# Gathers of a chunk set three tiles apart, and the slots of an element worked out three half products sooner, in a routed feed-forward kernel

## The chip, the cores and the metric

The kernel runs on one core of a Trainium2 chip. The metric is device time in microseconds (us) of one execution. The engines are PE (TensorE: products and transposes; PEld is its weight load), DVE (VectorE), ACT (ScalarE), POOL (GpSimd, which issues the gathers and scatters) and SP (SyncE, which issues most other transfers). A letter q behind an engine's name means its queue of issued transfers. Transfers of all queues are carried out by 16 DMA engines.

## The reference

For 16 elements (b) of 512 tokens by 512 numbers, a conditioned layer with a GELU is followed by a routed feed-forward layer. Each token goes to the 4 of 16 experts (blocks of 128 hidden units) with the largest router values; their results are added to the token and to a bias.

```python
def _L0_cond_ref(x, u, v, b, W, fc_bias):
    z1 = jnp.einsum('bfi,bir->bfr', x, v[:, 0]) / inch
    z = jnp.einsum('bfr,bor->bfo', z1, u[:, 0]) / r
    y = jnp.einsum('bfi,oi->bfo', x, W) + fc_bias + z + b
    return jax.nn.gelu(y, approximate=False)
...
prob = jax.nn.softmax(xf @ w_router + b_router, axis=-1)
_, idx = jax.lax.top_k(prob, TOP_K)
mask = (idx[:, :, None] == jnp.arange(N_BLOCKS)[None, None, :]).any(axis=1)
...
h = jax.nn.relu(jnp.einsum('nd,ebd->neb', xf, w1b) + b1b[None])
y = jnp.einsum('neb,ebd,ne->nd', h, w2b, mask)
y = y + b2[None, :]
...
x = x + _L0_ffn_ref(_L0_cond_ref(...), ...)
```

All of it is in float32.

## The kernel before

**What is stored where.** Every expert has a list of rows in `g_d` (device memory). A token's activated row, 512 numbers, is written into the lists of its four experts at positions called slots; results come back to the same slots of `y_d`. A slot is known once the router's choice is ranked among all earlier tokens.

**First stage (lines 758 to 773).** `window(b)` (L578) runs once for each of the 16 elements. It consists of eight half products, `cond_half(b, h)` (L255): two of the four products that make one quarter of the conditioned layer for element b; after each odd one ACT applies the GELU into `gT`. Between the halves stand other pieces of work, listed by half in `do[h]`:

- for element b+1: `weights` (L233, PE products `pw` and four DVE additions `we`), and four times `turn_x` (L245: four PE transposes into `ptx`, copied by DVE into `xT`);
- for element b+2: `spread_v`, `turn_v` and `turn_v_out` (PE transposes `pu`, copied by DVE and ACT), and the load of its x, which can start when the last `turn_x` of element b has read the buffer;
- for the element before, a = b-1: `logits_in` (L281, products `pa`, copied by ACT into `parts`), `logits` (L291, `pl`), `route_in` (L298: DVE, then the exponential on ACT), `route` (L307: some twenty small DVE operations from `sm`, L318, to `acc`, L350), `turn_g` for each of its four chunks of 128 tokens (L353: transposes `ptg`, copied into `gr` by DVE for odd chunks, by ACT for even ones), `rank` (L413: three small products `pp`, which need `acc`) and `place` (L427: DVE operations that end in `slot`, L441);
- in windows 5, 6, 7, 9 and 13 to 15 chores of DVE (`fill`, `count`, `take`, `table_ahead`, `table_part`), which count the lists' tiles and are put at halves 1, 3 and 6;
- two scatters `put` (L445) of a quarter of a chunk's rows each, which POOL issues. There are 16 for an element. In window b they belong to element b-2, and each waits for the half product before it.

Each engine works through its instructions in this order. `ptx`, `ptg` and half of `pw` share two PSUM buffers, so a transpose waits until the one two before has been copied. `gr` has two buffers for each chunk.

**Second stage (lines 782 to 798).** The lists are read as 271 full or partly full tiles of 128 rows. Step i fetches tile i+4 (L631, SP), turns tile i+1 (L649, copied by ACT into `gs`, L650), does the first product of tile i (L656, then ACT's `h`, L660) and the second of tile i-1 (L666, copied by ACT into `y`, L667, stored by SP, L668), and picks the weights of tile i+2 (L643, DVE). The first 22 tiles (`AHEAD`) are known to be full from the first elements alone, and can be read while later rows are still being put; tile 22 and all later ones wait for all puts, and for five scatters of zeros (`put_zero`, L499) that fill the ends of the lists. The puts that the first stage didn't do, and the zeros, are planned into the first steps (L751 to L755).

**The way back.** The tokens of an element come back in four chunks of 128, 64 chunks in all. `begun(b, c)` (L677) says after how many tiles a chunk's rows have all been worked out: with n = 4b+c+1, max(38, 4n+15). A chunk needs four gathers `get_y` (L690, POOL, 256 KB each, into two halves `yg`), a load of x (L682, issued by ACT, into one of 11 buffers), an addition of the bias (L707), two additions for each half (L710, L714), and a store (L717, SP). `plan(step, ...)` puts each behind a step, counted from `at`: the gathers at `at` to `at+3`, the load at `at-24`, the bias at `at+3`, the four additions at `at+4` to `at+7`, the store at `at+7`. POOL is not held to the steps: it issues a gather as soon as its turn has come, the stores of the chunk's tiles have landed and a `yg` buffer is free (there are six, so three chunks' worth). SP, ACT and DVE issue theirs in the place that the plan gives.

Of the kernel before, what the change touches and what calls it, by code (L numbers as in the profile page):

```python
# [19 lines left out]
TOP_K = 4  # L20
# [5 lines left out]
def adaln_ffn_kernel(  # L26
# [31 lines left out]
    B, S, D = x.shape  # L58
# [3 lines left out]
    NC = S // P  # L62
# [29 lines left out]
    def alone(ins):  # L92

        tc.declare_no_dep(ins.ins, group="put_g", reason="disjoint rows of the lists")
        tc.declare_no_dep(ins.ins, group="get_g", reason="the tiles that run ahead are full")
        tc.add_to_no_dep_group("put_g", ins.ins)
# [158 lines left out]
    def cond_half(b, h):  # L255

        o = h // 2
        if h % 2 == 0:
            pms[o] = ps_m.tile([P, S], F32, tag="m", name=f"pc_{b}_{o}")
        for k in range(h % 2 * ND // 2, (h % 2 + 1) * ND // 2):  # L260
            ins = nc.tensor.matmul(  # L261
                pms[o], lhsT=wes[b][:, k, o * P : (o + 1) * P], rhs=xTs[b, k], start=(k == 0), stop=(k == ND - 1)
            )
        if h % 2:
            gelu(b, o, pms[o])
        return ins
# [178 lines left out]
    def put(b, c, j, after):  # L445

        ins = nc.gpsimd.indirect_dma_start(  # L447
            out=g_d[:, :],
            out_offset=bass.IndirectOffsetOnAxis(ap=slot[:, b, c, j : j + 1], axis=0),
            in_=grs[b, c].bitcast(I32),  # L450
            in_offset=None,
        )
        tc.add_manual_dep(ins.ins, after.ins.name, SYNC, reason="spread over the products")
        alone(ins)
        if b < Q:
            early.append(ins.ins)
# [42 lines left out]
    def put_zero(i, after):  # L499
        ins = nc.gpsimd.indirect_dma_start(  # L500
            out=g_blocks if i else g_d[:, :],
            out_offset=bass.IndirectOffsetOnAxis(ap=zero_i[:, i : i + 1], axis=0),
            in_=(zero if i else zero[:, 0:D]).bitcast(I32),
            in_offset=None,
            bounds_check=NSLOT // ZB - 1 if i else NSLOT - 1,
            oob_is_err=False,
        )
        tc.add_manual_dep(ins.ins, after.ins.name, SYNC, reason="spread over the products")
        alone(ins)
# [65 lines left out]
    for k in range(known):  # L575
        chores.setdefault(B - 2 + k // 3, []).append(parts_of[k])

    def window(b):  # L578
        a = b - 1
        do = [[] for _ in range(2 * ND)]  # L580
        if b + 1 < B:
            do[0] += [(weights, b + 1)]
            do[2] += [(turn_x, b + 1, 0), (turn_x, b + 1, 1)]
            do[4] += [(turn_x, b + 1, 2), (turn_x, b + 1, 3)]
            if b > 0:
                do[1] += [(logits_in, a)]
                do[3] += [(logits, a), (route_in, a)]
                do[4] += [(route, a)]
                do[5] += [(turn_g, a, 0), (turn_g, a, 1)]
                do[6] += [(turn_g, a, 2), (turn_g, a, 3)]  # L590
                do[7] += [(rank, a), (place, a)]
            if b + 2 < B:
                do[2] += [(spread_v, b + 2)]
                do[5] += [(turn_v, b + 2), (turn_v_out, b + 2)]
        else:
            do[0] += [(logits_in, a)]
            do[1] += [(logits, a), (route_in, a)]
            do[2] += [(turn_g, a, 0), (turn_g, a, 1), (route, a)]
            do[3] += [(turn_g, a, 2), (turn_g, a, 3)]
            do[5] += [(rank, a), (place, a)]  # L600
        for h, what in zip((1, 3, 6), chores.get(b, ())):
            do[h] += [what]
        for h in range(2 * ND):
            ins = cond_half(b, h)
            for what, *args in do[h]:
                what(*args)
            if b > 1:
                for j in (0, 1):
                    put(b - 2, h // 2, h % 2 * 2 + j, ins)
            if later:  # L610
                what, *args = later.pop(0)
                what(*args)
# [4 lines left out]
    rows, gts, wcs, gss, hTs, mark, stores = {}, {}, {}, {}, {}, {}, []  # L617
# [59 lines left out]
    def begun(b, c):  # L677

        n = b * NC + c + 1
        return max(AHEAD + E, n * PB // NC + E - 1)  # L680
# [40 lines left out]
    GAP = 3  # L721
# [4 lines left out]
    def plan(step, *what):  # L726
        work.setdefault(step, []).append(what)

    for b in range(B):
        for c in range(NC):  # L730
            at = max(begun(b, c) + GAP, at + TOP_K if b + c else 0)
            k = b * NC + c
            soon = FREE - 2 * XA + 2 * k if k < XA else FREE + 4 + k - XA
            plan(soon if k < XA + XB else max(at - 24, soon), load_x, b, c)
            for j in range(TOP_K):
                plan(at + j, get_y, b, c, j)
            plan(at + LAND, sum_b, b, c)
            for h in range(2):
                plan(at + LAND + 1 + 2 * h, sum_y, b, c, h)
                plan(at + LAND + 2 + 2 * h, sum_x, b, c, h)  # L740
            plan(at + LAND + 4, store, b, c)


    z = B - 1
    for step, *what in (
        (-1, logits_in, z), (0, logits, z), (0, route_in, z), (1, turn_g, z, 0), (1, turn_g, z, 1), (1, route_a, z),
        (2, route_b, z), (2, turn_g, z, 2), (3, route_c, z), (3, turn_g, z, 3), (4, rank, z), (5, place, z),
        (6, count, B // Q - 1), (7, ends), *((8 + k, *w) for k, w in enumerate(parts_of[known:])), (8 + NTC, table, 1),
    ):
        plan(step, *what)  # L750
    for i in range(NC * TOP_K):  # L751
        for k, b in enumerate((z - 1, z)):
            plan(8 * k + i // 2, lambda b, c, j: put(b, c, j, mark[0]), b, i // TOP_K, i % TOP_K)
    for i in range(1 + NZ):
        plan(16 + i // 3, lambda i: put_zero(i, mark[0]), i)  # L755

    ENG = mybir.EngineType
    with tc.manual_schedule(engines={ENG.PE, ENG.DVE, ENG.Activation}):
# [10 lines left out]
        for b in range(B):  # L769
            if 2 <= b + 2 < B:  # L770
                load(b + 2)
            window(b)
# [76 lines left out]
```

## Time and profile before

| | |
|---|---|
| three timed runs | 1089.81, 1096.34, 1098.36 us |
| median | 1096.34 us |
| the profiled execution, its own time | 1086.83 us |
| its span, first to last instruction | 1085.1 us |
| mean granted TensorE clock | 0.967 |
| busy share of the span: PE, DVE, ACT, POOL | 89%, 60%, 48%, 51% |
| moved, mean | 342.43 MB, 316 GB/s |
| second products (tiles) | 271 |
| scatters and gathers of POOL | 256 and 256, and 5 of zeros |
| first tile transposed | at 387.21 us |
| last second product ends | at 1049.69 us |

The page's second part cuts the span into 40 slices of about 27 us; a digit is a busy share in tenths.

```profile
PE   5998988988999888789799999999999999999960
DMA  9966667566654469988799999999999999999996
GB/s 301 332 230 216 224 215 261 208 225 242 226 223 179 170 224 318 358 265 272 259 382 405 394 388 403 391 394 395 395 397 401 395 396 398 380 405 398 392 354 211
```

The first stage is slices 1 to 14. From slice 21 on the transfers run at about 395 GB/s, until the last two slices. The profiled execution is one of several and was faster than the three timed ones; sums from the profile are made against its own time.

### The profile page before, as it was taken

What the parts mean: (1) busy time and instruction counts of PE and PEld (TensorE: products, weight loads), DVE (VectorE), ACT (ScalarE), POOL (GpSimd) and SP (SyncE); (2) the same over time, 40 slices, a digit from 0 to 9 for tenths busy, and PEclk for the clock granted to TensorE, in tenths of its full rate; (3) what the DMA queues carried; (4) which work ended last, traced back from release to release, by engine and by line L of the source; (5) the groups of instructions that cost most, each with busy time, mean ns of one, the idle gap of its engine ahead of it and who ended that gap; (6) DMA issues with size and microseconds to landing.
All of it is one profiled execution on the core that took longest, in us unless ns stands there. A gap on an engine that the chain in (4) does not pass through costs nothing.

```text
span 1085.1 us, 19007 instructions
## 1 busy us (share of the span) xinstructions
PE 970.9 (89%) x5320; PEld 639.3 (59%) x5320; DVE 648.0 (60%) x1450; ACT 518.8 (48%) x1006; POOL 550.3 (51%) x538
## 2 busy tenths in 40 slices
PE   5998988988999888789799999999999999999960
PEld 3544444544444455567577677677767777777740
DVE  4365667566556767323366666566666666666675
ACT  2333332342333434456466666566656566666640
POOL 2046666666666667500454445455444454444555
PEclk9999999999999988989899999999999999999985
DMA  9966667566654469988799999999999999999996
GB/s 301 332 230 216 224 215 261 208 225 242 226 223 179 170 224 318 358 265 272 259 382 405 394 388 403 391 394 395 395 397 401 395 396 398 380 405 398 392 354 211
DMA packets 161480, 342.43 MB, mean 316 GB/s; under 512 B 28723, under 2 KB 36951, under 8 KB 159046
## 3 DMA queue, kind: packets, MB, share of 16 engines
q1 hardware_dynamic: 110928, 188.53, 48.1%
q0 software_dynamic: 41856, 136.96, 33.6%
q10 hardware_dynamic: 8592, 15.73, 4.1%
q8 instruction: 44, 0.72, 0.3%
q14 instruction: 60, 0.49, 0.1%
HBM read 179.91 MB, written 163.32 MB: 316 GB/s over the span
## 4 chain that ended last, share of the span: by engine, by line
PE 58%; DMA 19%; DVE 8%; issue 5%; ACT 3%; POOL 2%; SPq 2%; another core or an unknown queue 2%; ACTq 1%; DVEq 0%; POOLq 0%
PE pc L261 17%; DMA gt<-g_d 14%; PE ph L656 14%; PE py L666 13%; PE pts L649 6%; PE ptx L248 2%; PE ptg L357 2%; PE pw L241 2%; PE pa L285 1%; ACT gs L650 1%; PE pl L294 1%; DVE xT L250 1%; DMA yg<-y_d,slot 1%; POOL g_d L447 1%
## 5 line engine op out<-in xcount | busy, mean ns | idle before, releaser
L694 POOL DMA_INDIRECT yg<-y_d,slot x256 | 283.1, 1106 | 338.0 <-DVE xr L715 163.8
L643 DVE COPY wcur<-wall 128x1028 f32 x271 | 193.0, 713 | 271.1 <-PE py L666 164.0
L447 POOL DMA_INDIRECT g_d<-gr,slot x256 | 254.3, 993 | 185.2 <-issue 65.8
L656 PE MATMUL ph<-gs,wcur 128*128 128x128 f32 x2168 | 293.7, 279 | 17.7 <-ACT gs L650 9.8
L666 PE MATMUL py<-wcur,h 128*128 128x512 f32 x542 | 281.2, 601 | 5.5 <-ACT h L660 4.8
L656 PEld LDWEIGHTS ph<-gs,wcur 128*128 128x128 f32 x2168 | 266.8, 194 | 26.6 <-ACT gs L650 17.4
L261 PE MATMUL pc<-xT,we 128*128 128x512 f32 x512 | 246.3, 608 | 0.0
L649 PEld LDWEIGHTS pts<-ident,gt 128*128 128x128 f32 x1084 | 134.9, 143 | 165.2 <-issue 108.8
L667 ACT COPY y<-py 128x512 f32<-128x512 f32 x271 | 159.2, 587 | 94.0 <-PE py L666 69.5
L650 ACT COPY gs<-pts 128x512 f32<-128x512 f32 x271 | 160.0, 590 | 85.0 <-DMA gt<-g_d 39.6
L649 PE MATMUL pts<-ident,gt 128*128 128x128 f32 x1084 | 165.6, 276 | 16.4 <-DMA gt<-g_d 14.3
L660 ACT ACTIVATE h<-ph,wcur 128x128 f32<-128x128 f32 x271 | 100.0, 369 | 89.6 <-PE ph L656 43.0
L261 PEld LDWEIGHTS pc<-xT,we 128*128 128x128 f32 x512 | 88.4, 192 | 88.7 <-issue 88.7
L270 ACT ACTIVATE gT<-pc,biasT 128x512 f32<-128x512 f32 x64 | 44.0, 688 | 158.0 <-PE pc L261 101.8
L712 DVE TENSOR_TENSOR yg<-yg 128x512 f32<-128x512 f32 x128 | 87.3, 682 | 8.2 <-DMA yg<-y_d,slot 6.8
L666 PEld LDWEIGHTS py<-wcur,h 128*128 128x128 f32 x542 | 83.2, 194 | 6.8 <-ACT h L660 5.1
L250 DVE COPY xT<-ptx 128x512 f32<-128x512 f32 x64 | 42.0, 686 | 60.4 <-PE ptx L248 27.8
L715 DVE TENSOR_TENSOR xr<-xr,yg 128x512 f32<-128x512 f32 x112 | 76.6, 684 | 0.0
L357 PE MATMUL ptg<-ident,gT 128*128 128x128 f32 x256 | 37.8, 281 | 27.1 <-issue 9.8
L357 PEld LDWEIGHTS ptg<-ident,gT 128*128 128x128 f32 x256 | 30.0, 143 | 50.5 <-issue 24.9
L243 DVE TENSOR_TENSOR we<-pw,wc 128x512 f32<-128x512 f32 x64 | 40.1, 683 | 23.9 <-PE pw L241 16.2
L248 PEld LDWEIGHTS ptx<-ident,x 128*128 128x128 f32 x256 | 31.3, 146 | 18.3 <-issue 14.9
(159 smaller groups left out, 511.2 us busy)
## 6 DMA issues: line engine op xcount, KB each, us to landing
gt<-g_d SPq DMA_DIRECT2D x271, 256.0 KB
y_d<-y SPq DMA_DIRECT2D x271, 256.0 KB
x<-in_x_dram SPq DMA_DIRECT2D x16, 1024.0 KB
xr<-in_x_dram ACTq DMA_DIRECT2D x56, 256.0 KB
out_dram<-xr SPq DMA_DIRECT2D x56, 256.0 KB
wall<-in_w1T_dram SPq DMA_DIRECT2D x16, 256.0 KB
wall<-in_w2T_dram SPq DMA_DIRECT2D x16, 256.0 KB
g_d<-gr,slot POOLq DMA_INDIRECT x256
```

The costliest lines, as they stand in the source:

```text
L261: ins = nc.tensor.matmul(pms[o], lhsT=wes[b][:, k, o * P : (o + 1) * P], rhs=xTs[b, k], start=(k == 0), stop=(k == ND - 1))
L357: nc.tensor.transpose(pt[:, k, :], gTs[b, k][:, c * P : (c + 1) * P], ident)
L447: ins = nc.gpsimd.indirect_dma_start(out=g_d[:, :], out_offset=bass.IndirectOffsetOnAxis(ap=slot[:, b, c, j : j + 1], axis=0), in_=grs[b, ...
L643: nc.vector.tensor_copy(wcs[i], wall_f[:, bass.DynSlice(w, WW)])
L649: nc.tensor.transpose(pt[:, k, :], gts[i][:, k * P : (k + 1) * P], ident)
L650: nc.scalar.copy(gs.rearrange("p k t -> p (k t)"), pt.rearrange("p k t -> p (k t)"))
L656: mark[0] = nc.tensor.matmul(ph, lhsT=wcs[i][:, k * P : (k + 1) * P], rhs=gss[i][:, k, :], start=(k == 0), stop=(k == ND - 1))
L660: nc.scalar.activation(h, ph, AF.Relu, bias=wcs[i][:, ND * P : ND * P + 1])
L666: nc.tensor.matmul(py, lhsT=hTs[i], rhs=wcs[i][:, ND * P + 4 : WW], start=True, stop=True)
L667: nc.scalar.copy(y, py)
L694: ins = nc.gpsimd.indirect_dma_start(out=ygs[b, c, j // 2][:, j % 2, :].bitcast(I32), out_offset=None, in_=y_d[:, :], in_offset=bass.Indir ...
L712: nc.vector.tensor_tensor(yg[:, 0, :], yg[:, 0, :], yg[:, 1, :], ALU.add)
```

## The change

Three places are edited.

1. `window(b)` gets another order. The logits of element b-1 come at halves 0 and 1 (1 and 3 before), its route at 2 (4), rank and place at 4 (7), `turn_g` at 4, 6, 7 and 7 (5, 5, 6, 6). The weights of b+1 come at half 3 (0), its `turn_x` at 1, 5, 5 and 6 (2, 2, 4, 4). The last window gets the same order, where it had one of its own.
2. The puts start earlier. Half h of window b issues puts 2h and 2h+1 of a sequence in which the first `LAG` = 10 are the last ten of element b-2, and the other six the first six of element b-1. Behind the first stage ten puts of the last but one element are left, at steps 0 to 4 (16 before, at steps 0 to 7); those of the last element stand at steps 6 to 13 (8 to 15), and all five zeros at step 14 (16 and 17).
3. Chunks stand 3 steps apart, instead of 4, until the other bound (`begun + GAP`) holds. The four gathers stand at `at`, `at`, `at+1`, `at+2`. All that is counted from `at` moves with it.

```diff
+    LAG = 10
+
+    def puts_of(b, i, after):
+        if b >= 0:
+            put(b, i // TOP_K, i % TOP_K, after)
+
     def window(b):
         a = b - 1
         do = [[] for _ in range(2 * ND)]
-        if b + 1 < B:
-            do[0] += [(weights, b + 1)]
-            do[2] += [(turn_x, b + 1, 0), (turn_x, b + 1, 1)]
-            do[4] += [(turn_x, b + 1, 2), (turn_x, b + 1, 3)]
-            if b > 0:
-                do[1] += [(logits_in, a)]
-                do[3] += [(logits, a), (route_in, a)]
-                do[4] += [(route, a)]
-                do[5] += [(turn_g, a, 0), (turn_g, a, 1)]
-                do[6] += [(turn_g, a, 2), (turn_g, a, 3)]
-                do[7] += [(rank, a), (place, a)]
-            if b + 2 < B:
-                do[2] += [(spread_v, b + 2)]
-                do[5] += [(turn_v, b + 2), (turn_v_out, b + 2)]
-        else:
+        if b > 0:
             do[0] += [(logits_in, a)]
             do[1] += [(logits, a), (route_in, a)]
-            do[2] += [(turn_g, a, 0), (turn_g, a, 1), (route, a)]
-            do[3] += [(turn_g, a, 2), (turn_g, a, 3)]
-            do[5] += [(rank, a), (place, a)]
+            do[2] += [(route, a)]
+            do[4] += [(rank, a), (place, a), (turn_g, a, 0)]
+            do[6] += [(turn_g, a, 1)]
+            do[7] += [(turn_g, a, 2), (turn_g, a, 3)]
+        if b + 1 < B:
+            do[1] += [(turn_x, b + 1, 0)]
+            do[3] += [(weights, b + 1)]
+            do[5] += [(turn_x, b + 1, 1), (turn_x, b + 1, 2)]
+            do[6] += [(turn_x, b + 1, 3)]
+        if b + 2 < B:
+            do[2] += [(spread_v, b + 2)]
+            do[5] += [(turn_v, b + 2), (turn_v_out, b + 2)]
...
-            if b > 1:
-                for j in (0, 1):
-                    put(b - 2, h // 2, h % 2 * 2 + j, ins)
+            for i in range(2 * h, 2 * h + 2):
+                puts_of(b - 2 + (i >= LAG), (i - LAG) % (NC * TOP_K), ins)
...
-            at = max(begun(b, c) + GAP, at + TOP_K if b + c else 0)
+            at = max(begun(b, c) + GAP, at + 3 if b + c else 0)
...
-                plan(at + j, get_y, b, c, j)
+                plan(at + 3 * j // TOP_K, get_y, b, c, j)
...
+    for i in range(LAG):
+        plan(i // 2, lambda i: puts_of(z - 1, i, mark[0]), NC * TOP_K - LAG + i)
     for i in range(NC * TOP_K):
-        for k, b in enumerate((z - 1, z)):
-            plan(8 * k + i // 2, lambda b, c, j: put(b, c, j, mark[0]), b, i // TOP_K, i % TOP_K)
+        plan(6 + i // 2, lambda i: puts_of(z, i, mark[0]), i)
     for i in range(1 + NZ):
-        plan(16 + i // 3, lambda i: put_zero(i, mark[0]), i)
+        plan(14, lambda i: put_zero(i, mark[0]), i)
```

## The prediction

> **What bounds the kernel now.** I read the windows by stage first, then the waits, then the timeline at three places. In the windows the columns are stretch, length, busy microseconds (and instructions) of PE, PEld, DVE, ACT, POOL, then the granted clock, DMA share and GB/s.
>
> ```profile
> 278.00:302.00 24.00, 22.02 (x103) 11.08 (x95) 13.66 (x44) 8.50 (x13) 15.69 (x17) 1.00 0.62 223
> 410.00:440.00 30.00, 24.03 (x128) 16.77 (x127) 20.47 (x69) 12.90 (x27) 20.56 (x19) 0.89 0.91 319
> 440.00:470.00 30.00, 19.74 (x118) 15.06 (x117) 6.02 (x9) 11.94 (x26) 11.13 (x10) 0.83 0.86 314
> 470.00:520.00 50.00, 49.90 (x318) 37.58 (x316) 15.22 (x22) 31.43 (x66) 5.87 (x6) 1.00 0.87 289
> 700.00:900.00 200.00, 194.57 (x1210) 143.26 (x1210) 124.60 (x194) 123.13 (x262) 97.53 (x86) 1.00 1.04 396
> 1040.00:1085.00 45.00, 9.69 (x56) 6.56 (x54) 30.45 (x46) 6.56 (x14) 25.64 (x25) 0.63 0.80 261
> ```
>
> The first stage is TensorE's: 22 of 24 us busy, DMA at 0.62. From 700 to 900 DMA is full (396 GB/s, share 1.04) and TensorE nearly so: the ACT h rows of the timeline give 2.305 us a tile (653.12 for tile 98, 1026.59 for tile 260) against 2.19 where DMA has room (tiles 22 to 41). The last 45 us have DMA room.
>
> ```profile
> 293.52 0.69 DVE L359 COPY gr<-ptg 128x512 f32<-128x512 f32 x1
> 294.27 0.65 PE L357 MATMUL ptg<-ident,gT 128*128 128x128 f32 x4 [1.83 <-issue]
> ...
> 453.96 1.05 POOL L500 DMA_INDIRECT g_d<-zero,zero_i  x1 [0.31 <-issue]
> 462.61 4.85 SPq L631 DMA_DIRECT2D gt<-g_d  x6
> 465.34 1.09 PE L649 MATMUL pts<-ident,gt 128*128 128x128 f32 x4 [10.14 <-DMA gt<-g_d]
> ...
> 512.34 1.00 POOL L694 DMA_INDIRECT yg<-y_d,slot  x1 [57.33 <-DMA y_d<-y]
> ...
> 1074.77 1.32 POOL L694 DMA_INDIRECT yg<-y_d,slot  x1 [0.30 <-issue]
> 1079.94 0.69 DVE L712 TENSOR_TENSOR yg<-yg 128x512 f32<-128x512 f32 x1 [1.95 <-DMA yg<-y_d,slot]
> ```
>
> Timeline rows: start, length, engine, line, [idle before]. Three costs show: a PE hole of 1.83 us in a window, because the copy of gr at 293.52 stands behind the route chain; one of 10.14 us between the stages, because the fetch of tile 22 waits for the last zero; and the tail, where 19 gathers follow PE's last product (1049.69), one each 1.27 us.
>
> ```profile
> 868.14 7.50 DMA gt<-g_d
> ...
> 1074.77 5.08 DMA yg<-y_d,slot
> ```
>
> The chain of waits gives a landing: 7.5 us with full queues, 5.1 us in the tail.
>
> **The change part by part.**
>
> *First stage, usual windows.* No product is added. The PE holes before the L357 and L241 rows of the eight windows without a chore (1, 2, 3, 4, 8, 10, 11, 12) add up to 0.62+1.45+2.84+0.79+2.61+0.97+1.83+1.84 = 12.9 us. In the new order the first to wait for the route chain is rank. From the end of pl, PE has until rank: one turn_x 0.5, two halves 3.4, the weights 1.07, a half 1.9 = 6.9 us. DVE and ACT need: pr to the subtraction 0.85, xT 0.69 (table load and exp beside it, 1.5 in all), then the 4.6 us from sm (288.88) to acc's end (293.48): 6.2 us. Slack 0.7, so no hole. After it the weights' four additions (2.5) and place (1.55) end at 10.3; the second and third turn_x are ready to be copied then, and turn_g finds its buffers free. I take -12.9. If the slack fails by 1 us (parts was copied 1.6 to 2.0 us after pa's end in four windows), this term is near 0.
>
> *First stage, windows with a chore.* A chore now stands on DVE between the logits and the route, or between the weights and place. A count is 4.25 us (231.62 to 235.83): rank waits 10.5-6.9 = 3.6, turn_g 0.4 more. Windows 7, 9, 13: 4.0 each, for 0.76, 2.64, 2.09 now: +6.5. Windows 5 and 6 (fill or take, then a count or table at half 3): place and the copies of xT end 4 us later, turn_g waits 4.2: +0.7 and +1.2. Window 14 (table parts of 2.5): +1.2. The last: rank waits 2.5, +2.5. In all +12.1. Bounds 0 and +20.
>
> *Queues in it.* SP's load of x for b+2 waits for the fourth turn_x, at half 6 instead of 4: 5 us later, and the clears and weight loads queue behind it; the load still has about 30 us until it is turned, and DMA is at 0.62: nothing, and PE stands for each us past those 30. POOL's put 0 at half 5 waits for slot (10.3 against the product's 9.4): 0.9 us, for 1.5 of slack beside 16 puts at 1.27 = 20.3 in 21.8. The gr buffers now have 11 halves to be emptied, for 8.
>
> *Between the stages.* Last zero at 453.96 now. After: 10 puts are left for steps 0 to 4, and 16 start when slot is there (414.3, unchanged); step 13's product ends at 438.6, so its pair ends at 441.2, and five zeros at once (1.3 to 1.5 each, as now) issue the last at 446.9. That is 7.1 earlier, and the fetch, SP's y stores behind it and PE's 10.14 us hole follow: -7.1. Bounds 0 (something else holds step 13) and -9. The hole's end ran slow: 1.09 for four transposes that take 0.60. The Trainium skill's page "TensorE: Matmul & The Clock Gate" (Part 1) has the clock halve after an idle window of about 3.4 us; a hole of 3 us would by that spare the slow restart, some 1.5 us by the rows at 465. The profile has shorter holes with clock 0.89 too (410 to 440), so I leave it out: 0, with -1.5 kept in the range.
>
> *Gathers three apart.* Chunk n (from 1) stands at step max(4n+18, 38+3n) for 37+4n: from n = 20 it follows its tiles by 3 steps; the last is at 274 for 293. Each moves its four gathers (0.26 MB each), its additions, its x load (ACT) and its store (SP). DMA is full there, so bytes moved forward cost their time: 1050 to 1085 carried 8.4 MB (the 5 us windows); with four gathers, two y, three stores and what is in flight, about 2.9 stay. 5.5 MB at 395 GB/s = +13.9. Tail: now 35.4 (1049.69 to 1085.1); after: y copied and issued 1.4, landed 4, four gathers 4.9 to the last one's end less 1.0, landing 5.2, two additions 1.4, store 4.2 = 20.1: -15.3. From 530 to 550 DMA runs at 255 GB/s; one more half chunk is freed there: 0.5 MB, -1.3. Together -2.7.
>
> *A new wait on ACT.* Load k waits until the store of chunk k-11 has left its buffer. While three apart, load comes 2 steps after that store (13 now). Store: SP lag 1.2, landing 7.5 = 8.7, against 5.3: ACT waits up to 3.4 for some ten chunks, with the copies of gs, h and y, so PE, behind it. PE has 3 x (2.65-2.19) = 1.4 to spare per chunk there, and shorter queues shorten the landing. Between 0 and +20; I take +2, as DMA stays fed by fetches under way.
>
> *A new wait on DVE.* The first addition of yg stands 7 steps after its tile's y copy: 7 x 2.305 + 0.9 = 17.1 us. The first gather started 6.0 us after that copy with queues not full (506.34 to 512.34); full, I add 2.4 = 8.4; second gather 1.3 later, landing 7.5: 17.2. On time within 0.1. DVE's next pick is needed at 21.4 and takes 0.7 after the addition's 0.7, so 2.9 us late costs PE nothing. The skill's page "DMA: Bandwidth & Descriptors" (Anatomy of one DMA) gives a DMA 2.0 us plus its bytes over 436e3, which makes 2.6 for a gather, an estimate: by that it lands 5 us earlier, the wait can't arise and the tail is 4 shorter. The rows decide, for there 7.5 and 5.1 were taken. I take +1; bounds 0 and the rival below.
>
> Sum: -12.9+12.1-7.1-2.7+2+1 = -7.6 us. The profiled execution took 1086.83, so 1079; it stands 9.5 below the median, so on the median 1089.
>
> **The rivals.** *Gathers too close to their tiles (slower).* Place: DVE at L712, from chunk 20 on. If y store and gather together take over 2.9 us more than 17.2, pick is late in each of 44 chunks. At 4 late, PE loses 1.1, of which 0.5 is DMA's share (4 x 0.115): 0.6 x 44 = +26, so 1115. For: SP's issue lags up to 2.4 us. Against: shorter queues land sooner.
>
> *The middle has room after all (faster).* If TensorE and not DMA holds the 2.305, the +13.9 falls away: 1075. For: PE 97% busy. Against: 395 GB/s unchanged for 400 us.
>
> *The spacing doesn't come.* Only six yg buffers: POOL's gathers wait for the additions (163.8 us in all <-DVE xr L715). But the additions are moved with the plan, so buffers come earlier too. If it failed, only the stage part is left: 1088.
>
> **How the numbers follow.** 1% (11 us) is about what can be told from no change. Likeliest with its variant of no spacing 0.48 (range 1080 to 1100), slower 0.32, which also has the lost slack before rank and ACT's wait, faster 0.20. Of the first 0.12 lies below 1085 and 0.02 above 1107; of the slower 0.27 above; of the faster 0.13 below. Faster 0.25, same 0.46, slower 0.29. Eight in ten: 1070 to 1116.
>
> **What would show it.** No PE hole at turn_g in usual windows and one of 3 to 4 us before rank at a count; the last zero near 447 and a hole of 3 us after; 395 GB/s from 545 on, at 2.6 us a tile until about tile 98; a tail near 20 us. Wrong if DVE waits over 3 us at L712 in every chunk, or ACT stands long before L689.

## The result, and the profile after

| | before | after |
|---|---|---|
| median of 6 runs | 1095.48 us | 1145.72 us |
| lowest to highest | 1089.81 to 1100.15 | 1142.53 to 1154.36 |
| profiled execution, its span | 1085.1 us | 1144.3 us |
| tile 0's h starts (L660) | 393.2 | 439.8 |
| from there: tiles 0 to 22 | 77.3 | 69.0 |
| tiles 22 to 41 | 41.6 | 41.6 |
| tiles 41 to 98 | 141.0 | 157.7 |
| tiles 98 to 270 | 394.9 | 412.1 |
| last tile's h to the end | 37.0 | 24.1 |

The ratio is 1.0473, 95% interval 1.0422 to 1.0525: slower by 50 us, where 7 us faster was predicted. The table's differences are +46.6, -8.3, 0, +16.7, +17.2 and -12.9, in sum +59.3; the two spans differ by 59.2. The profiled execution of the kernel before was some 9 us faster than its median, so the table shows more than the 50 us. The first stage makes most of it.

By stretches (stretch, length, busy us and instructions of PE, PEld, DVE, ACT, POOL, clock, DMA share, GB/s), the changed kernel:

```profile
27.00:440.00 413.00, 359.34 (x1468) 181.53 (x1466) 226.63 (x748) 124.25 (x184) 225.65 (x231) 0.94 0.58 206
...
84.00:121.00 37.00, 25.10 (x96) 12.88 (x95) 13.65 (x44) 9.38 (x14) 21.90 (x23) 0.82 0.53 192
...
700.00:900.00 200.00, 189.33 (x1163) 138.74 (x1164) 121.09 (x190) 117.20 (x251) 89.60 (x84) 1.00 1.03 385
```

and the kernel before over its first stage:

```profile
27.00:393.00 366.00, 335.58 (x1459) 171.64 (x1458) 229.56 (x745) 123.84 (x183) 216.81 (x222) 1.00 0.63 226
```

The first row of each covers nearly the same products (nine records more after). TensorE is idle 413.00-359.34 = 53.7 us for 30.4, so 23 of the 47 us are new holes. The other 24 are busy time, 359.34 for 335.58. Some 15 of them are the lower clock (0.94 for 1.00), an estimate: busy time times the missing share of the clock, summed over stretches of 4 us, is 16.2 us after and 1.3 before. The stretch with the longest hole (84 to 121) has 0.82. Another 7 are waits that count as busy, in the products `pw` (below).

**Where the holes are.** The PE rows of the first stage, by group (busy us, mean ns, idle before them and its releasers); the changed kernel, from 40 to 450 us:

```profile
L357 PE MATMUL ptg<-ident,gT 128*128 128x128 f32 x256 | 38.6, 285 | 8.2 <-DVE xT L250 4.8 <-issue 1.8 <-DVE we L243 1.6
...
L241 PE MATMUL pw<-us,uT 16*128 16x512 f32 x112 | 23.0, 642 | 1.1 <-issue 1.0
...
L294 PE MATMUL pl<-pick,parts 128*128 128x16 f32 x128 | 16.4, 261 | 12.4 <-issue 11.2 <-ACT parts L289 1.2
...
L417 PE MATMUL pp<-acc,ones 128*128 128x80 bf16 x15 | 3.1, 204 | 28.5 <-DVE acc L350 28.5
```

and the kernel before in the same view:

```profile
L357 PE MATMUL ptg<-ident,gT 128*128 128x128 f32 x256 | 37.8, 281 | 27.1 <-issue 9.8 <-DVE gr L359 8.1 <-ACT gr L361 5.2
...
L241 PE MATMUL pw<-us,uT 16*128 16x512 f32 x112 | 16.0, 639 | 0.8 <-issue 0.8
```

The turns of g (L357) have 8.2 us of idle time, for 27.1: that hole was removed as planned. In its place stand 28.5 before rank, for none, and 12.4 before the logits, for none. Of the 28.5, 4.9 lie in usual windows and 23.7 in windows with a chore. `pw` is busy for 23.0 us instead of 16.0: in seven windows most of its eight products begin only 0.05 us after DVE's copy `xT` has ended, so that it takes up to 2.3 us instead of 1.14 (2.20 at 314.71, with a clock of 1.00 there). A usual window of the changed kernel (timeline: start, length, engine, line, idle before):

```profile
286.80 0.96 PE L294 MATMUL pl<-pick,parts 128*128 128x16 f32 x8
...
289.50 0.22 DVE L300 TENSOR_TENSOR pr<-pl,br 128x64 f32<-128x64 f32 x1 [6.44 <-PE ptx L248]
...
295.14 0.77 DVE L350 TENSOR_TENSOR acc<-acc,mask 128x16 bf16<-128x16 bf16 x4
...
295.96 0.20 PE L417 MATMUL pp<-acc,ones 128*128 128x80 bf16 x1 [1.22 <-DVE acc L350]
```

pl ends at 287.76, pr waits for nothing else that the profile shows, and starts at 289.50: 1.74 us late. From pr to acc's end it takes 6.4 us, and rank waits 1.22. In window 3 the copy of parts is late, in the same trace:

```profile
85.26 1.04 PE L285 MATMUL pa<-gT,wr_g 128*32 128x512 f32 x2 [0.17 <-ACT gT L270]
...
98.73 0.58 ACT L289 COPY parts<-pa 128x512 f32<-128x512 f32 x1 [11.50 <-remote]
99.37 1.89 PE L294 MATMUL pl<-pick,parts 128*128 128x16 f32 x8 [11.15 <-issue]
```

ACT's last work before had ended at 87.2, pa at 86.3. "remote" means that no event of the profile explains the release; the copy waits on TensorE's semaphore alone. The hole of 11.15 follows at once, and the next eight 16-column products take 1.89 us for 0.96; the granted clock is 0.50 from 100 to 104. This window, with the clock behind the hole, is 34.4 us long for 24.6 before.

**Between the stages and behind.** The changed kernel's last zero and the first turn that waits behind it, that of tile 22:

```profile
488.42 0.96 POOL L500 DMA_INDIRECT g_d<-zero,zero_i  x1 [0.30 <-issue]
...
502.20 1.09 PE L649 MATMUL pts<-ident,gt 128*128 128x128 f32 x4 [4.24 <-DMA gt<-g_d]
```

The hole is 4.24 us for 10.14, and its end still runs slow (1.09 for 0.60, with a clock of 0.50 from 502 to 506). Of the gathers, the waits say:

```profile
POOL yg L694 <- DMA y_d<-y: 93.2, 25, 7.3
...
POOL yg L694 <- DVE xr L715: 42.5, 15, 8.5
DVE yg L712 <- DMA yg<-y_d,slot: 23.8, 18, 5.3
```

(total, times, longest.) POOL now waits most for the tiles' stores, and 42.5 us for buffers instead of 163.8: the gathers do follow their tiles. DVE waits for a gather 18 times, not in each chunk. The tail of the changed kernel:

```profile
1130.54 0.95 POOL L694 DMA_INDIRECT yg<-y_d,slot  x1 [4.85 <-DMA y_d<-y]
```

Seven gathers follow the last second product (it ends at 1121.81), for 19 before. The row is the first of the last chunk's four, which waited for the store of y.

### The profile page after: what moved, and what is told of

Same layout as the page of the kernel before. It is cut to its first block, busy times and chain, and to the rows that moved or that the text cites. A ratio compares the mean times of both kernels' runs of the same rounds, so it can differ in the third digit from the quotient of the medians.

```text
span 1144.3 us, 19015 instructions
## 1 busy us (share of the span) xinstructions
PE 996.8 (87%) x5320; PEld 649.5 (57%) x5320; DVE 639.8 (56%) x1450; ACT 516.1 (45%) x1006; POOL 540.9 (47%) x538
## 3 DMA queue, kind: packets, MB, share of 16 engines
q1 hardware_dynamic: 110928, 188.53, 46.6%
## 4 chain that ended last, share of the span: by engine, by line
PE 68%; DVE 12%; DMA 10%; issue 5%; ACT 2%; SPq 1%; DVEq 0%; another core or an unknown queue 0%; POOL 0%; ACTq 0%; POOLq 0%
PE ph L656 18%; PE py L666 16%; PE pc L261 16%; PE pts L649 8%; DMA gt<-g_d 5%; PE ptg L357 3%; PE ptx L248 2%; DMA y_d<-y 2%; DMA yg<-y_d,slot 1%; PE pa L285 1%; ACT gs L650 1%; PE pl L294 1%; DVE ti L326 1%; DVE xT L250 1%; DVE we L243 1%
## 5 line engine op out<-in xcount | busy, mean ns | idle before, releaser
L694 POOL DMA_INDIRECT yg<-y_d,slot x256 | 276.2, 1079 | 369.7 <-DMA gt<-g_d 130.4
L656 PE MATMUL ph<-gs,wcur 128*128 128x128 f32 x2168 | 294.6, 279 | 33.6 <-ACT gs L650 23.7
L261 PE MATMUL pc<-xT,we 128*128 128x512 f32 x512 | 254.2, 628 | 0.0
L660 ACT ACTIVATE h<-ph,wcur 128x128 f32<-128x128 f32 x271 | 100.3, 370 | 123.5 <-PE ph L656 49.9
L261 PEld LDWEIGHTS pc<-xT,we 128*128 128x128 f32 x512 | 93.9, 201 | 101.6 <-issue 97.8
L712 DVE TENSOR_TENSOR yg<-yg 128x512 f32<-128x512 f32 x128 | 87.6, 684 | 25.6 <-DMA yg<-y_d,slot 23.8
L270 ACT ACTIVATE gT<-pc,biasT 128x512 f32<-128x512 f32 x64 | 44.0, 687 | 101.5 <-PE pc L261 85.1
L300 DVE TENSOR_TENSOR pr<-pl,br 128x64 f32<-128x64 f32 x16 | 3.6, 225 | 102.1 <-PE pc L261 52.2
L361 ACT COPY gr<-ptg 128x512 f32<-128x512 f32 x32 | 18.6, 582 | 80.5 <-PE ptg L357 66.7
L357 PEld LDWEIGHTS ptg<-ident,gT 128*128 128x128 f32 x256 | 30.3, 145 | 28.8 <-issue 12.5
L359 DVE COPY gr<-ptg 128x512 f32<-128x512 f32 x32 | 22.1, 690 | 44.0 <-PE ptg L357 27.5
```

The lines of the kernel that those rows point to most:

```text
L261: ins = nc.tensor.matmul(pms[o], lhsT=wes[b][:, k, o * P : (o + 1) * P], rhs=xTs[b, k], start=(k == 0), stop=(k == ND - 1))
L656: mark[0] = nc.tensor.matmul(ph, lhsT=wcs[i][:, k * P : (k + 1) * P], rhs=gss[i][:, k, :], start=(k == 0), stop=(k == ND - 1))
L660: nc.scalar.activation(h, ph, AF.Relu, bias=wcs[i][:, ND * P : ND * P + 1])
L694: ins = nc.gpsimd.indirect_dma_start(out=ygs[b, c, j // 2][:, j % 2, :].bitcast(I32), out_offset=None, in_=y_d[:, :], in_offset=bass.Indir ...
L712: nc.vector.tensor_tensor(yg[:, 0, :], yg[:, 0, :], yg[:, 1, :], ALU.add)
```

## The experiments

They ran in five groups, each on one chip with its own runs of the kernel before. That kernel took 1060.98 and 1062.58 us in A and D (chip 1 on record), 1091.35 and 1088.10 in B and C (chip 15), 1087.36 in E (chip 0). Chip 1 is called the prompt chip below, for the reason that the traces of A give; the others are called late. The chip of the first result is not on record; its traces are of the late kind. Ratios are within a group. "Chores late" moves the chores of DVE to the end of the window, "rank late" puts rank and place one half later.

| group | kernel | median us | ratio, 95% interval |
|---|---|---|---|
| A | order alone | 1064.86 | 1.0027 (1.0011 to 1.0044) |
| A | spacing alone | 1080.31 | 1.0154 (1.0107 to 1.0200) |
| A | changed, chores late | 1049.84 | 0.9882 (0.9838 to 0.9925) |
| A | changed, rank late | 1078.96 | 1.0188 (1.0129 to 1.0247) |
| B | changed, again | 1147.26 | 1.0519 (1.0496 to 1.0541) |
| B | order alone, chores late | 1105.64 | 1.0139 (1.0106 to 1.0171) |
| B | spacing alone, 7 behind | 1112.66 | 1.0167 (1.0111 to 1.0224) |
| C | left-over puts earlier | 1088.06 | 0.9995 (0.9978 to 1.0013) |
| C | that, turns and chores later | 1088.19 | 1.0010 (0.9989 to 1.0031) |
| C | order alone, again | 1119.44 | 1.0317 (1.0242 to 1.0393) |
| C | spacing alone, again | 1107.77 | 1.0145 (1.0084 to 1.0206) |
| D | changed, chores late, again | 1051.61 | 0.9907 (0.9876 to 0.9937) |
| D | order alone, chores and rank late | 1040.98 | 0.9796 (0.9762 to 0.9829) |
| D | that, logits late too | 1064.77 | 1.0033 (1.0016 to 1.0050) |
| E | order alone, chores and rank late, again | 1099.67 | 1.0120 (1.0088 to 1.0152) |
| E | changed, again | 1134.77 | 1.0452 (1.0410 to 1.0495) |

The kernel before was also profiled once in B (1096.93) and once in D (1062.17).

**One part at a time (A).** Order alone keeps the spacing (this edit of the changed kernel), spacing alone keeps window order and puts (the reverse edit of the kernel before):

```diff
-            at = max(begun(b, c) + GAP, at + 3 if b + c else 0)
+            at = max(begun(b, c) + GAP, at + TOP_K if b + c else 0)
...
-                plan(at + 3 * j // TOP_K, get_y, b, c, j)
+                plan(at + j, get_y, b, c, j)
```

> The new order of the window, the earlier puts and the new plan of the last puts, with chunks four steps apart as before. Theory (the order of the first stage carries most of the loss: tile 0 came 46.6 us later in the profile after, the gap between the stages gave 8.3 back): 38 us slower than before, ratio about 1.035. Rival (the spacing carries it, by keeping transfers full): ratio under 1.01.

> Only the spacing of the chunks; window and puts as before. Theory by the tile times of the profile after (17 us between tiles 41 and 98, 17 between 98 and 270, 13 gained in the tail): 20 us slower than before, ratio about 1.019. Rival, the forecast's own term (bytes moved forward cost what the tail gains): within 4 us of before.

The second met its expectation nearly (1.015 for 1.019). The first missed: 1.003 for 1.035. The trace of order alone says why. Window 3, where the changed kernel had its hole of 11 us:

```profile
82.78 0.96 PE L294 MATMUL pl<-pick,parts 128*128 128x16 f32 x8
...
83.78 0.22 DVE L300 TENSOR_TENSOR pr<-pl,br 128x64 f32<-128x64 f32 x1 [4.74 <-PE pl L294]
...
88.86 0.77 DVE L350 TENSOR_TENSOR acc<-acc,mask 128x16 bf16<-128x16 bf16 x4
...
90.48 0.20 PE L417 MATMUL pp<-acc,ones 128*128 128x80 bf16 x1
```

pr starts 0.04 us after pl, acc ends at 89.63, rank waits for nothing. From window 2 on, windows without a chore take 21.1 us; those of the kernel before take 22.2 or 22.3 on that chip (its trace in D). Rank still waits 12.9 us in all, only in windows with a chore. pr is 0.04 us late in every window, where in the changed kernel's own trace it was 0.9 to 3.6 late in nine of sixteen. Both cannot come from the code. The kernel before shows the same on its own, hidden: window 5, first from the trace that the prediction read:

```profile
134.46 1.06 PE L285 MATMUL pa<-gT,wr_g 128*32 128x512 f32 x8
...
137.11 0.59 ACT L289 COPY parts<-pa 128x512 f32<-128x512 f32 x1 [1.86 <-remote]
```

and then from spacing alone in A, which has the same window:

```profile
131.48 1.07 PE L285 MATMUL pa<-gT,wr_g 128*32 128x512 f32 x8
...
132.64 0.59 ACT L289 COPY parts<-pa 128x512 f32<-128x512 f32 x1 [0.36 <-PE pa L285]
```

1.59 us after pa's end against 0.09, the same instructions around it. So the lateness comes with the chip, or with the program's state on it, and not with the instructions.

**Moving the chores, or rank (A).** In the changed kernel:

```diff
-        for h, what in zip((1, 3, 6), chores.get(b, ())):
+        for h, what in zip((7, 7, 7) if b < B - 2 else (5, 6, 7), chores.get(b, ())):
```

```diff
-    LAG = 10
+    LAG = 12
...
-            do[4] += [(rank, a), (place, a), (turn_g, a, 0)]
+            do[4] += [(turn_g, a, 0)]
+            do[5] += [(rank, a), (place, a)]
```

> The changed kernel with DVE's chores at the end of the window (half 7; halves 5, 6, 7 in the last two), where DVE has nothing that a product waits for. Theory (chores ahead of the route make rank's holes of 5 us, and each such hole makes TensorE run at a lower clock for a while): the seven windows with chores get 24 us or less for 26 to 31, about 30 us faster than the changed kernel, ratio to before near 1.02. Rival (the late start of pr is enough by itself, chores or not): under 10 us faster.

> The changed kernel with rank and place one half later (5 instead of 4) and the first puts of an element one half later too (LAG 12). Theory (rank is reached before the route chain ends): its holes shrink by 1.9 us in each of 15 windows, 20 to 30 us faster than the changed kernel with the clock's share, ratio to before about 1.02 to 1.03. Rival (another wait comes next, the copies behind place on DVE): under 10 us faster.

Chores late took the chore windows to 21.1 as well, tile 0 to 360.4 (order alone: 383.0), and the whole below the kernel before, where 1.02 had been expected from the first result. Rank late alone took the wait before rank from 12.9 to 0.2 us, but left the chore windows at 24.6 to 26.9, with 19.9 us of idle time at the turns: its rival had named another wait that comes next.

**A late chip (B, C).** The changed kernel again, the kernel before for its trace, and order alone with the chores late (both edits above):

> The changed kernel, unaltered, beside the parts of it. Theory (the order's loss depends on how late DVE starts pr after pl, which was 0 to 3.6 us in the profile after and near 0 in the order alone): the parts add up here, 0.3% and 1.5%, ratio near 1.02, and usual windows of 21.1 us. Rival (the two parts harm each other): 1.047 as in the first result, with windows of 24 us.

> The kernel before, unaltered, for a profile beside those of its parts. Theory: windows of 22.3 us as in the spacing alone, rank about 1.9 us after the route chain's last copy is freed, tail of 37 us, a hole near 10 us before tile 22. Rival: windows of 23 to 25 us as in the first profile before.

> The new order and the earlier puts, chores at the end of the window, chunks four steps apart as before. Theory (the order is a gain once the chores are out of its way: windows of 21.1 us for 22.3 to 25, and the last zero 7 us earlier; the spacing is a loss): the chores' variant of the changed kernel had 0.988, less 1.5% of the spacing: 0.973. Rival (the late chores only helped beside the new spacing): 0.985 to 0.99.

> The window order, the earlier scatters and the earlier left-over scatters alone, spacing of four as before; 1.003 was measured where the kernel before took 1061. Theory (the new order costs what it does by DVE and ACT starting late after TensorE, which differs from chip to chip): where the kernel before takes 1061 again, 1.003 again, with each pr of DVE 0.04 us after the end of pl; where it takes 1090 or more, 1.03 to 1.04, with pr up to 3.6 us late and 25 us or more of PE idle before rank. Rival (the lateness comes with the three-step spacing or differs from run to run): 1.003 to 1.01 on any chip.

The rival won for the first: 1.052, with pr late by 2.1 to 3.1 us in seven windows. The kernel before also came nearer to its rival, with windows of 22 to 28 us. Order with chores late missed: 1.014 for 0.973. Order alone met its conditional expectation, 1.032, and this is the decisive pair: the same kernel costs 0.3% on one chip and 3.2% on another, in its timed runs. In the second its pr is 2.3, 3.2 and 2.6 us late in three windows and 0.9 in two, ACT stands 13.5 before parts once, idle before rank 23.6 and before pl 12.9.

**Spacing (B, C).** Three apart, but seven steps behind the tiles, in the kernel before:

```diff
-            at = max(begun(b, c) + GAP, at + TOP_K if b + c else 0)
+            at = max(begun(b, c) + (GAP if b + c == 0 else 7), at + 3 if b + c else 0)
```

> Before with chunks three steps apart, but following their tiles by 7 steps instead of 3 once they have caught up. Theory (the loss between tiles 98 and 270 comes from gathers that stand too close to their tiles' stores): that stretch costs what it does before, the tail some 5 us more than with 3; ratio near 1.00 where the spacing alone has 1.015. Rival (bytes moved forward are what costs): 1.012 or more.

> The spacing of three alone, window order and scatters as before; 1.015 was measured where the kernel before took 1061. Theory (spacing costs through DMA alone, which does not depend on the chip): 1.012 to 1.02 again on any chip, tiles 41 to 98 about 15 us longer, tiles 98 to 270 15 to 20 us longer, the tail 13 shorter. Rival (the gathers close to their tiles are hurt by the late starts too): 1.025 or more where the kernel before takes 1090.

Spacing alone cost 1.5% on both kinds of chip. Within C, against order alone: tiles 41 to 98 took 162.1 for 140.9 us, 98 to 270 403.1 for 394.7, the tail 25.1 for 38.0. One sign of the prediction's slower rival did come: DVE waits for gathers in many more places than in the first trace after, most on the prompt chip (spacing alone, A):

```profile
DVE yg L712 <- DMA yg<-y_d,slot: 76.8, 49, 7.8
```

In C it is 49.9 us in 36 waits. Seven steps behind took it down to 7.7 us in 4 waits and cost as much (1.017), so on the late chip neither this wait nor the nearness of gathers to their tiles is the cause. On the prompt chip TensorE waited 16.2 us for DVE's pick, for 7.0 in the kernel before; there the wait may have a share.

**The hole between the stages alone (C).** The left-over puts and zeros earlier, in the kernel before:

```diff
-            plan(8 * k + i // 2, lambda b, c, j: put(b, c, j, mark[0]), b, i // TOP_K, i % TOP_K)
+            plan((6 * k) + i // 3, lambda b, c, j: put(b, c, j, mark[0]), b, i // TOP_K, i % TOP_K)
...
-        plan(16 + i // 3, lambda i: put_zero(i, mark[0]), i)
+        plan(12, lambda i: put_zero(i, mark[0]), i)
```

> The kernel before with its window order and its spacing; only the scatters that are left behind the first stage are planned earlier: those of the last two elements at steps i//3 and 6+i//3, and all zeros at step 12. Theory (the scatters left over, not the order of the windows, set the hole between the stages): the last zero comes some 8 us earlier, so tiles 0 to 22 take about 69 us instead of 76 to 77, and the rest is unchanged: ratio 0.992, between 0.990 and 0.995. Rival (the scatters held by POOL's pace of 1.27 us and by the slot of the last element, so that an earlier step gives nothing): tiles 0 to 22 as before, ratio 0.999 to 1.001.

The hole shrank as meant (timeline of this kernel), and the time did not move:

```profile
465.72 0.63 PE L649 MATMUL pts<-ident,gt 128*128 128x128 f32 x4 [1.40 <-DMA gt<-g_d]
```

1.40 us is left of the 10.14, but holes of 1.8, 2.9 and 3.9 us stand in the first tiles; tiles 0 to 22 took 73.4, for 76.4 in that chip's trace of the kernel before (B) and 69 expected. The ratio is the rival's, the reason is not: the zeros did come earlier. Where the rest went isn't settled.

**Turns and chores later, long way to rank (C).** On top of the last edit, with the chores at half 7 except in the last two windows:

```diff
-                do[5] += [(turn_g, a, 0), (turn_g, a, 1)]
-                do[6] += [(turn_g, a, 2), (turn_g, a, 3)]
-                do[7] += [(rank, a), (place, a)]
+                do[5] += [(turn_g, a, 0)]
+                do[6] += [(turn_g, a, 1)]
+                do[7] += [(rank, a), (place, a), (turn_g, a, 2), (turn_g, a, 3)]
```

> As the run with earlier left-over scatters, and in the windows the kernel before's long way from the logits (half 3) to the rank (half 7) is kept, while the four turns of g stand at halves 5, 6, 7 and 7 (5, 5, 6, 6) and the chores at half 7. Theory (the turns' wait behind the route chain can be taken away without putting rank close to the logits): the PE idle time at the turns falls from 30 us to under 10, no idle time comes before rank, the first stage gets 15 to 20 us shorter on either kind of chip, ratio 0.975 to 0.98. Rival (DVE is the stage's second bound, so its delay shows at the next instruction of PE that needs it, at the weights or the turns of x of the next window): the stage gets less than 8 us shorter, ratio 0.985 to 0.992.

The rival had the mechanism: idle time at the turns fell from 28.1 to 7.5 us and came back at the weights (12.2 for 0.6). The ratio, 1.001, is above both forecasts.

**Longer ways in the new order (D, E).** Order alone with chores and rank late (the two edits above), then with the logits at half 2, the route at 3, rank and place at 6 and LAG 14:

> The changed kernel with its chores at half 7 (in the last two windows at 5, 6, 7); 0.988 was measured where the kernel before took 1061. Theory (order without chores costs 1.4% by late starts where the kernel before takes 1090, the spacing another 1.5%): 1.025 to 1.035 there, and 0.985 to 0.99 again where it takes 1061. Rival (the chores alone made the loss): below 1.01 on any chip.

> The changed order with spacing four, chores at half 7, and rank and place at half 5 instead of 4 (the scatters two later, LAG 12). The way from pl to rank is one half (1.9 us) longer. Theory (late starts turn into idle time where the way is short): where the kernel before takes 1090, the idle time before rank falls below 5 us (9.3 us with rank at 4), that before pl (way from pa, unchanged) stays at 10 to 25 us, ratio 1.00 to 1.01, against 1.014 with rank at 4. Rival (the order is slow there whatever the distances): 1.014 or more.

> As the run with both late, but with the logits at half 2 (1) and rank and place at half 6 (LAG 14): both ways are one half longer still or again. Theory: idle time before pl below 8 us and before rank below 5 us, the first stage as short as before or shorter, ratio 0.98 to 1.00 where the kernel before takes 1090. Rival (idle time moves to the next instruction that needs DVE, the turns or the weights): 1.005 or more, with the same sum of idle time as with both late.

> The kernel before, for its trace beside the other runs of this call. Both theories: its usual time within 0.5%; first stage 393 to 400 us where it takes 1090, near 375 to 380 where it takes 1061, and starts of pr 0.04 us after pl in every window only in the latter.

> The changed order with chores at half 7 and rank and place at half 5, spacing four; 0.980 was measured where the kernel before took 1063. Theory (short ways turn late starts into idle time): 0.98 again there; where the kernel before takes 1090, idle time before rank below 5 us, that before pl 10 to 25 us, ratio 1.00 to 1.01. Rival (distance does not matter): 1.014 or more where it takes 1090.

> The changed kernel as it is. Theory (the order costs 0.3% where engines start promptly and 3.2% where they start late, the spacing 1.5% on both, and they add up): 1.015 to 1.025 where the kernel before takes 1060, 1.045 to 1.055 where it takes 1090. Rival (order and spacing hurt each other): 1.03 or more where it takes 1060.

D fell on the prompt chip. The kernel before met its expectation there (tile 0 at 378.9, pr 0.04 us late in every window), and so, nearly, did the changed kernel with chores late (0.991). Chores and rank late with the old spacing is the fastest version there, 0.980, every interval from rank to rank but the last two 21.1 us. Against it the changed kernel with chores late is 10.6 us slower; the two differ in the spacing and in rank's half. The longest ways lost all of it: windows of 22.8, 19.8 us of idle time at the turns, as the rival of that run had it. E came on a late chip. On another late chip (B) the PE groups of order alone with chores late had been

```profile
L357 PE MATMUL ptg<-ident,gT 128*128 128x128 f32 x256 | 37.6, 279 | 8.0 <-DVE gr L359 5.2 <-issue 1.8 <-DVE xT L250 0.6
L294 PE MATMUL pl<-pick,parts 128*128 128x16 f32 x128 | 17.5, 270 | 22.0 <-issue 16.0 <-ACT parts L289 6.0
L417 PE MATMUL pp<-acc,ones 128*128 128x80 bf16 x16 | 3.2, 198 | 8.0 <-DVE acc L350 8.0
```

and in E, with rank late too, they were:

```profile
L357 PE MATMUL ptg<-ident,gT 128*128 128x128 f32 x256 | 39.0, 281 | 19.1 <-DVE gr L359 8.3 <-DVE we L243 5.6 <-DVE xT L250 3.8
L294 PE MATMUL pl<-pick,parts 128*128 128x16 f32 x128 | 16.9, 265 | 7.5 <-ACT parts L289 7.0 <-issue 0.5
L417 PE MATMUL pp<-acc,ones 128*128 128x80 bf16 x16 | 3.2, 199 | 0.0
```

The longer way takes the idle time before rank away altogether, as expected, but 11 us come back at the turns, and the ratio (1.012) can't be told from 1.014. Before pl, whose way was not changed, 14.5 us went too, so the two traces differ in lateness as well. That distance decides where lateness shows, and not whether it costs, is argued from this pair and not shown by it. The changed kernel itself was 1.045 in E, as expected for a late chip. It wasn't run on the prompt chip, where the sum of the two parts would be 1.018.

No version beat the kernel before on both kinds of chip: the best one gains 2.0% on the prompt chip and loses 1.2% on a late one.

## Why the prediction was wrong, step by step

**The failed step: "Slack 0.7, so no hole".** The prediction lets pr begin with the end of pl, and counts both terms of the first stage from there: no hole in a usual window, 3.6 us before rank with a count. The rest of that sum held. In the usual window shown, DVE took 6.41 us from pr to acc for 6.2, and TensorE came to rank 6.98 us after pl for 6.9. But pr began 1.74 us late, so rank waited 1.22. In the late traces of the changed kernel pr is up to 3.6 us late. From the last GELU of a window to that of the next (starts of L270; the last one to tile 0's h), the two terms came out so:

| | predicted | first traces | prompt chip, order alone (A) for before (D) |
|---|---|---|---|
| eight usual windows | -12.9 | 198.3 for 185.8: +12.5 | 168.0 for 177.9: -9.9 |
| seven windows with a chore | +12.1 | 202.3 for 169.2: +33.1 | 178.9 for 162.7: +16.2 |

Where pr does begin 0.04 us after pl, both terms stand within 3 to 4 us of the prediction, and usual windows have no hole. Where it begins late, each is 21 to 25 us worse than predicted. Why it begins late there is open.

**What was left out of the usual windows.** The prediction saw the sign (parts 1.6 to 2.0 us late in four windows) and took it as a risk that could only bring the term to 0. A lateness of 2 us in a chain with 0.7 of slack is 1.3 us of waiting. In four of these windows pr is 0.9 to 2.7 us late and rank waits 1.2 us, 4.9 together; part of the lateness goes into the waits of `pw`, 7 us over all windows, which the prediction had at 1.07 us a window with no wait. The way from pa to pl, one half of 1.9 us of which the copy of parts takes 0.6, was not worked out at all. It made 12.4 us before pl, 11.15 of them in window 3, which alone grew by 9.8 of the 12.5 us. That single copy started 12.4 us late; nothing in the trace before, whose latest was 2.0, could have told its size.

**Windows with a chore (+12.1, bounds 0 and +20).** Windows 5 and 6 became 8.6 us longer, 1.9 predicted for both; lateness and chore stand in one chain and add up: the three longest waits before rank are 5.2 to 5.4 us, for 2.6 to 2.9 on the prompt chip. That chores belong behind the chain is shown on that chip: tile 0 at 360.4 for 383.0.

**The clock.** The prediction weighed the Trainium skill's clock gate ("TensorE: Matmul & The Clock Gate", Part 1, a halved clock after an idle window of about 3.4 us) only for the hole between the stages. It belonged in the first stage, where the lower clock cost some 15 us. The holes there need not be that long:

```profile
160.00:164.00 4.00, 4.00 (x13) 1.94 (x12) 3.83 (x10) 1.07 (x2) 0.70 (x1) 0.60 0.34 131
...
272.00:276.00 4.00, 4.00 (x12) 1.84 (x10) 2.86 (x9) 0.82 (x2) 0.75 (x1) 0.57 0.34 131
```

These stretches of the changed kernel follow holes of 1.97 and 3.08 us before rank; after the one of 5.24 us the clock is 0.50 from 372 to 376. In the kernel before it stays at 1.00 from 104 to 108, after a hole of 2.84. So in these runs no single length of hole decides.

**Queues, POOL and SP.** Nothing was expected, and no row of SP's loads or of the gr buffers stands in the new chain. Right, as far as seen.

**Between the stages (-7.1).** Tiles 0 to 22: -8.3; within A, 67.1 with the new order and 74.1 with the old one. Right in size (the hole is 4.2 us, about 3 were expected), and the slow restart stayed, as assumed. That the same hole closed in another way gave no time (C) shows that this number is a stage's and not the whole kernel's.

**Three apart (-2.7).** Middle +12.6 predicted, +16.7 here and +21 in C; tail -15.3 predicted, -12.9 here. The direction of both is right, the sizes are off by 4 to 8 and by 2.4, against the change. **The waits on ACT and DVE (+2, +1).** In the first trace after, the waits list no ACT wait at the loads, and 23.8 us of DVE at L712 (6.8 before), part of them in the tail. Yet tiles 98 to 270 took 17.2 us longer (8.4 in C), at 385 GB/s for 396. This is the second step that failed: the prediction charged the moved bytes to the middle alone and the later stretch with 3 us of waits. Why it became longer is open. The rival (DVE late in each chunk) does not carry it on a late chip: 18 waits in the first trace, and seven steps behind, with 4 waits, cost the same. Taken by itself the spacing cost 1.5% on either kind of chip, where the three terms together made 0.3 us.

## What to carry to other kernels

Before a chain between engines is shortened, measure in the trace how late each of its links starts after its producer, over all rounds and not in one clean one, and take the slack against the worst; then add to the price of each hole what a lower clock behind it may cost (here some 15 us of clock to 23 us of new holes). Ask of every link, not only of the last one, what it costs if it is late. Put work that nobody waits for (chores) behind such a chain, not into it. A schedule tuned to a microsecond can win on one chip and lose on the next, so judge it on more than one.

## What the runs showed of the hardware that was not expected

The same kernel took 1061 us on one chip and 1087 to 1095 elsewhere. In the traces of the former, pr starts 0.04 to 0.5 us after pl and parts 0.09 to 0.12 us after pa in every window. In the others pr starts 1 to 3.8 us late in several windows (once 6.1), and parts up to 4.8 us, but 12.4 to 14.9 us late at one place of the new order: window 3, in three traces of the changed kernel and of order alone, and with chores late. A further trace of the changed kernel (B) has 4.6 us there, and that with rank late too has none. "remote" releases, some 14 to 31 in a trace on the late chips, are absent from the traces of the prompt chip. Some late places repeat for the same window order (parts of window 5 in the old one: 1.59, 1.56, 1.55 us, and 1.71 and 1.66 in C), others don't, on the same chip either (B and C are one chip). What holds the engines there was not found, and no run was made for it; only one prompt chip was met.
